# One attention and mixture-of-experts kernel: VectorE's order of gates, value differences and make-ahead work, and the place of the last key and value loads

## The chip, the core and the metric

The kernel runs on one core of a Trainium2 chip. The metric is the device time of one execution in microseconds; the median of several runs is compared. Five engines work side by side, each in the order in which its instructions were issued: TensorE (PE: matrix products, with PEld for its weight loads), VectorE (DVE), ScalarE (ACT), GpSimd (POOL) and SyncE (SP, here only the issuer of most DMAs). They wait for each other by semaphores.

## The reference

Two sequences of 2048 tokens with 512 features are normalised. One branch is causal attention over them, the other a mixture of 8 experts of which each token uses 2. The output joins both:

```
xn = layernorm(x)
q, k, v = split(layernorm(xn)*gamma + beta) @ qkv          # 512 each
s  = softmax(causal(q @ k.T / sqrt(512))) @ v @ o_proj + xn
g  = silu(sum over the 2 best experts e of  gate_e * (silu(xn @ w1_e.T + b1_e) @ w2_e.T + b2_e))
out = x + s * g
```

## The kernel before

**Stages.** All products are float32. The first stage (about 0 to 300 us) normalises, folds the weights into `wqk` and `wvo`, and writes keys `kt_d`, queries `qt_d` and values `v_d` to memory. The second (about 300 to 632 us) sorts tokens by expert, runs the experts and writes their outputs to `y_d`. The third (632 us to the end) is the attention and the final joining; the change lies there.

**The attention loop.** The main loop at the end of the kernel runs over steps `s`. There are NT = 32 tiles of 128 queries; `seq` orders them (sequence 0 from the last tile to the first, then sequence 1 in a mixed order that ends with its longest tiles). Keys and values stand in blocks of 512; `b` counts them, 0 to 3 for sequence 0 and 4 to 7 (`K` to `K + 3`) for sequence 1. Step s does, in the order in which the instructions are issued:

- scores of tile s on PE, one bank of PSUM for each block of keys (`chunk_scores`, L836). After each block DVE takes its maximum (L842), and then one of the previous tile's `join_p` copies (L924);
- `end_scores` makes the negative maximum `nm` of the tile (L854), `exponentials` has ACT exponentiate (L908), POOL split the result into 16-bit halves `pu` (L912) and SP turn them by DMA (`puT`, L917). The joins of the next step put the halves together to `pT`;
- `fetch_parts` issues loads on SP's queue, at most four a step: `parts_b` lists them by their step, keys (`fetch_k`), values (`fetch_v`) and queries (`fetch_q`), each key or value block in four parts of 256 KB;
- `gate(k)` (L1094, L1095): four DVE operations that weigh the experts' rows for two tiles, and a Silu on ACT (L1099). The rows come by POOL's `gather_y` (L1083);
- the product of probabilities and values, two steps behind the scores.

At the head of later steps `attended` scales a product (ACT L1104, DVE L1107) and `emit` multiplies with the gate and adds x on POOL (L1115, L1116). For the last two tiles (`AHEAD`), `make_ahead` (L1127 to L1129) prepares factors on DVE, and `emit_ahead` uses them.

**Two ways to multiply by the values.** Pairs of tiles not in `FAST` use `values(s)` (L942): products on PE alone. The pairs in `FAST` (pairs 0 to 3 and 13 to 15) use a scheme of the Strassen-Winograd kind with seven products for two tiles. It needs differences of the values, `combine_v` (L967: t1 to t4 for each block), and sums of the probabilities, `combine_p` (L986: s1, s3, s2, s4). `values_first` makes p12 and o1, `values_next` makes p57, both in the even step; `values_end`, in the odd step, makes p64 and p03. Between these products DVE adds parts (`add`, L1011). All of p12, p57, p64 and p03 are banks of one pool with three buffers (`ps_b`). In the odd step:

```
chain(p64[:, LO], s2, vt(s, 1))
add(u2, p64[:, LO], p1)        # DVE, reads the left half of p64
...
chain(p64[:, HI], a22, vt(s, 3), stop=False)
```

So PE's last chain in a pair writes the half of a bank whose other half the first `add` reads.

**Order.** The order is written by hand: the program is issued inside a manual schedule, and what is issued first on an engine runs first on it. In step 2, `combine_p` makes the value differences of all four blocks of sequence 0, each kind right after the sum with its number. Those of sequence 1 come in steps 20, 22, 26 and 29 (`combine`). The gate of pair k comes in step k + 3 (28: step 30; 30: step 31).

Of the kernel before, what the change touches and what calls it, by code (L numbers as in the profile page):

```python
# [26 lines left out]
def gated_attention_moe(  # L27
# [31 lines left out]
    NT = B * S // P  # L59
# [818 lines left out]
    for i in range(NS):  # L878
        experts_step(i)
        if i >= 8 and i % 2 == 0 and early:  # L880
            f, b, c = early.pop(0)
# [73 lines left out]
    def combine_v(b, parts=(1, 2, 3, 4)):  # L955

        n = 1 if b % NBB == NBB - 1 else 2
        v = avs[b].rearrange("p (i h) d -> p i h d", h=2)[:, :n]
        if 1 in parts:
            avts[b] = cp.tile(  # L960
                [P, n, 4, D // 2], F32, name=f"vT_{b}", tag=f"vT{n}", bufs=(1 if n == 1 else NBB - 1)
            )
        t1, t2, t3, t4 = (avts[b][:, :, i, :] for i in range(4))
        b11, b12, b21, b22 = (v[:, :, h, c] for h in range(2) for c in (LO, HI))
        for i, dst, x1, x2 in (1, t1, b12, b11), (2, t2, b22, t1), (3, t3, b22, b12), (4, t4, b21, t2):
            if i in parts:
                nc.vector.tensor_tensor(dst, x1, x2, ALU.subtract)  # L967

    def combine_p(s, blocks=()):


        m = min(place_keys(s), place_keys(s + 1)) // 2
        assert m < 2 * NBB
        a1, a2 = (
            turned[s + i][:, : 2 * m * P].rearrange("p (k h q) -> p k h q", h=2, q=P)
            for i in range(2)
        )
        a11, a12, a21, a22 = a1[:, :, 0], a1[:, :, 1], a2[:, :, 0], a2[:, :, 1]
        s1, s2, s4 = (
            cp.tile([P, 2 * NBB - 1, P], F32, name=f"s{i}_{s}", tag=f"s{i}")[:, :m] for i in (1, 2, 4)  # L980
        )
        for i, dst, x1, x2, op_ in (
            (1, s1, a21, a22, ALU.add), (3, a21, a11, a21, ALU.subtract),
            (2, s2, s1, a11, ALU.subtract), (4, s4, a12, s2, ALU.subtract),
        ):
            nc.vector.tensor_tensor(dst, x1, x2, op_)  # L986
            for b in blocks:
                combine_v(b, (i,))
        combos[s] = m, a11, a12, a22, s1, s2, a21, s4

    def chain(dst, a, v, stop=True):
# [36 lines left out]
    def values_next(s):  # L1028
        _, _, _, _, s1, _, s3, _ = combos[s]
        p57 = bank(s, "p57")  # L1030
        chain(p57[:, LO], s1, vt(s, 0))
        chain(p57[:, HI], s3, vt(s, 2))
        seven[s] += (p57,)
# [45 lines left out]
    def gather_y(s):  # L1079
        n = seq[s]  # L1080
        for k in range(2):
            y = op.tile([P, D], F32, name=f"yg{k}_{s}", tag=f"yg{k}")
            nc.gpsimd.indirect_dma_start(  # L1083
                out=y, out_offset=None, in_=y_d,
                in_offset=bass.IndirectOffsetOnAxis(ap=posi[k][:, n : n + 1], axis=0),
            )
            rows[s, k] = y

    def gate(s):

        g = op.tile([P, 2, D], F32, name=f"g_{s}", tag="g", bufs=2)
        for i in range(2):
            w = [share[k][:, 0, seq[s + i] : seq[s + i] + 1] for k in range(2)]
            nc.vector.tensor_scalar(g[:, i, :], rows.pop((s + i, 0)), w[0], None, ALU.mult)  # L1094
            nc.vector.scalar_tensor_tensor(  # L1095
                g[:, i, :], rows.pop((s + i, 1)), w[1], g[:, i, :], ALU.mult, ALU.add
            )
            gates[s + i].append(g[:, i, :])
        nc.scalar.activation(g, g, AF.Silu)  # L1099
# [23 lines left out]
    def make_ahead(s):  # L1123
        xt, g = gates[s]
        n = seq[s]
        w = op.tile([P, D], F32, name=f"w_{s}", tag="w", bufs=1)
        nc.vector.tensor_scalar(w, g, xscale[:, n : n + 1], 1.0, ALU.mult, ALU.add)  # L1127
        nc.vector.tensor_tensor(xt, xt, w, ALU.mult)
        nc.vector.scalar_tensor_tensor(  # L1129
            xt, g, xshift[:, n : n + 1], xt, ALU.mult, ALU.add  # L1130
        )

    def emit_ahead(s, o, cols):
# [9 lines left out]
    K = NBB  # L1143
    parts_b = [(0, fetch_v, 0), (0, fetch_v, 1), (1, fetch_v, 2), (1, fetch_v, 3),
               (4, fetch_k, K + 2), (6, fetch_v, K + 2), (8, fetch_k, K + 1), (10, fetch_v, K + 1),
               (12, fetch_k, K), (14, fetch_v, K), (16, fetch_k, K + 3), (18, fetch_v, K + 3)]
    parts_b = [(s, f, b, c) for s, f, b in parts_b for c in range(ND)]
    parts_b += [(2 * n - 2 * NQ + 2, fetch_q, n, c) for n in range(NQ, NT // 2) for c in range(2)]
    parts_b.sort(key=lambda part: part[0])
# [9 lines left out]
    for s in range(NT + OUT + 2):  # L1159
        fast = s // 2 - 1 in FAST  # L1160
        if s < NT and s:
            begin_scores(s)
        if s == 1:
            fetch_parts(s, 2 * ND)
        for k in range(NT):
            if k not in AHEAD:
                wait = 4 - k % 2 if k // 2 in FAST else 3
                if s == k + wait:
                    attended(k)
                if s == k + wait + 1:  # L1170
                    emit(k)
        for k in range(NT):
            if s == (NT - 1 if k in AHEAD else k + 2 - k % 2 if k // 2 in FAST else k + 1):
                fetch_inputs(k)
        joins = []
        if 0 <= s - 1 < NT - 1:
            joins = [(join_p, s - 1, j) for j in range(len(widths[s - 1]))]
        if s < NT:
            for j in range(len(widths[s])):
                if s:  # L1180
                    chunk_scores(s, j)
                if joins:
                    f, *args = joins.pop(0)
                    f(*args)
        for f, *args in joins:
            f(*args)
        if s < NT and s:
            end_scores(s)
        if fast and s % 2 == 0 and s < NT:
            combine_p(s - 2, range(NBB) if s == 2 else ())  # L1190
        if 0 <= s - 1 < NT:
            divisor(s - 1)
        if s < NT:
            exponentials(s)
            fetch_parts(s, 4 if s else 2 * ND)
            if s in combine:
                combine_v(combine[s])

        for k in range(0, NT, 2):
            if s == (k + 1 if k in AHEAD else k + 2 if k + 2 in AHEAD else k + 3):  # L1200
                gate(k)
        for k in range(0, NT, 2):
            if s == (k if k in AHEAD else k + 1):
                gather_y(k)
                gather_y(k + 1)
        if s == NT - 1:
            for k in AHEAD:
                make_ahead(k)
        if fast and s % 2 == 0:
            values_first(s - 2)  # L1210

            if s != NT - 2:
                values_next(s - 2)
        elif fast and s == NT - 1:
            values_next(s - 3)
            values_end(
                s - 3,
                [lambda j=j: join_p(s, j) for j in range(len(widths[s]))] + [lambda: combine_p(s - 1)],
            )
        elif fast:  # L1220
            values_end(s - 3)
        elif 0 <= s - 2 < NT:
            values(s - 2)
    att.close()


# [42 lines left out]
```

## Time and profile before

| what | value |
|---|---|
| median of 3 runs | 1093.47 us (1091.65 to 1094.91) |
| the profiled execution's own time | 1094.23 us |
| its span, first to last instruction | 1092.5 us |
| granted clock of TensorE | 0.998 of full speed |
| PE busy | 1068.2 us, 98% |
| DVE busy | 556.1 us, 51% |
| POOL busy | 401.8 us, 37% |
| ACT busy | 328.9 us, 30% |
| DMA | 210.08 MB, 192 GB/s in the mean |

Times in the profile are counted from the span's start. A row of a timeline gives start, length, engine, line, operation, the tile written and read, the count of merged instructions and, in square brackets, how long the engine stood idle before it and what it waited for. In the list of waits a row gives the waiting engine and line, what it waited for, the microseconds in total, how often, and the longest. A float32 product appears as two matmul instructions.

### The profile page before, as it was taken

How to read it: one execution, taken by the hardware profiler on the slowest of the kernel's cores; microseconds unless marked ns; L12 is line 12 of the kernel's file. 1: busy time of each engine (PE TensorE's matmuls, PEld its weight loads, DVE VectorE, ACT ScalarE, POOL GpSimd, SP SyncE). 2: the span in 40 equal slices, each digit the busy share in tenths (PEclk: the TensorE clock that was granted, in tenths of full speed). 3: DMA queues.
4: the chain of work that ended last, by engine and by line, in shares of the span. 5: the costliest groups of instructions: out<-in, count | busy, mean ns of one | idle time of the engine just before them, and what ended most of it. 6: DMA issues, size and time to landing. Idle time of an engine off the chain costs nothing.

```text
span 1092.5 us, 11592 instructions
## 1 busy us (share of the span) xinstructions
PE 1068.2 (98%) x3326; PEld 575.9 (53%) x3326; DVE 556.1 (51%) x1102; ACT 328.9 (30%) x689; POOL 401.8 (37%) x443
## 2 busy tenths in 40 slices
PE   8999999999999999999999999999999999999998
PEld 3444444444555555555545446676654444546567
DVE  4634441686333333333345338555565558675675
ACT  3232423211333232323256231221233333432230
POOL 2411120002433333333331023353557577673342
PEclk9999999999999999999999999999999999999999
DMA  8989879935999999999985175455668796663451
GB/s 298 250 248 285 253 229 333 307 108 139 183 255 224 228 226 226 236 223 232 207 187 148 34 226 143 90 123 150 156 185 211 221 240 194 177 164 89 98 127 38
DMA packets 306509, 210.08 MB, mean 192 GB/s; under 512 B 238088, under 2 KB 250888, under 8 KB 305424
## 3 DMA queue, kind: packets, MB, share of 16 engines
q1 hardware_dynamic: 284368, 146.91, 54.5%
q0 software_dynamic: 10560, 35.17, 12.7%
q10 hardware_dynamic: 11520, 27.27, 6.7%
q8 instruction: 28, 0.46, 0.2%
q14 instruction: 33, 0.27, 0.1%
HBM read 92.89 MB, written 60.03 MB: 140 GB/s over the span
## 4 chain that ended last, share of the span: by engine, by line
PE 80%; issue 6%; DVE 5%; POOL 5%; ACT 2%; DMA 2%; ACTq 0%; POOLq 0%; DVEq 0%
PE ps L836 15%; PE py L791 15%; PE ph L752 15%; PE pj L324 10%; PE pj L329 9%; PE p L994 8%; PE pw L200 3%; PE po L942 3%; POOL yg L1083 2%; POOL o L1115 1%; DMA puT<-pu 1%; PE p L942 1%; DVE g L1094 1%; POOL o L1116 1%; PE pg L290 1%
## 5 line engine op out<-in xcount | busy, mean ns | idle before, releaser
L836 PE MATMUL ps<-k,q 128*128 128x512 f32 (+3 forms) x640 | 239.1, 529 | 0.0
L791 PE MATMUL py<-w,ht 128*128 (+3 forms) x408 | 187.0, 594 | 0.0
L836 PEld LDWEIGHTS ps<-k,q 128*128 128x128 f32 x640 | 117.9, 190 | 121.8 <-issue 111.7
L752 PE MATMUL ph<-w,xT 128*128 (+1 forms) x544 | 173.1, 460 | 0.7 <-POOL keep L874 0.7
L912 POOL COPY pu<-pr 128x1024 uint16<-128x1024 uint16 (+3 forms) x80 | 89.3, 1142 | 198.5 <-ACT pr L908 177.6
L777 ACT ACTIVATE ht<-ht,b1sel 128x128 f32<-128x128 f32 (+3 forms) x237 | 73.1, 375 | 230.6 <-DVE ht L771 230.6
L752 PEld LDWEIGHTS ph<-w,xT 128*128 128x128 f32 (+1 forms) x544 | 97.5, 181 | 73.0 <-issue 33.1
L799 DVE COPY y<-py 128x512 f32<-128x512 f32 x68 | 46.9, 690 | 173.7 <-PE py L791 173.7
L762 POOL COPY hu<-h 128x704 uint16<-128x704 uint16 x68 | 52.5, 772 | 206.7 <-ACT h L760 153.4
L324 PE MATMUL pj<-kT,wqk 128*128 128x512 f32 x256 | 113.2, 595 | 0.0
L791 PEld LDWEIGHTS py<-w,ht 128*128 128x128 f32 (+3 forms) x408 | 73.6, 182 | 75.1 <-issue 38.3
L329 PE MATMUL pj<-wvo,kT 128*128 128x512 f32 x256 | 113.0, 595 | 0.0
L638 POOL DMA_INDIRECT xs<-zu_d,toki x68 | 69.4, 1020 | 69.3 <-DVE toki L538 57.9
L908 ACT ACTIVATE pr<-ps,nm 128x512 f32<-128x512 f32 (+3 forms) x80 | 49.0, 620 | 151.4 <-DVE ri L1067 137.9
L842 DVE TENSOR_REDUCE mx<-ps 128x1 f32<-128x512 f32 (+3 forms) x80 | 48.7, 609 | 78.6 <-PE ps L836 77.4
L942 PE MATMUL po<-v,pT 128*128 128x512 f32 x182 | 83.1, 604 | 5.0 <-DVE ri L1067 2.8
L334 ACT COPY j<-pj 128x512 f32<-128x512 f32 x64 | 37.3, 583 | 141.6 <-PE pj L324 66.7
L324 PEld LDWEIGHTS pj<-kT,wqk 128*128 128x128 f32 x256 | 47.7, 190 | 59.1 <-issue 54.9
L247 POOL COPY zu<-z 128x1024 uint16<-128x1024 uint16 x32 | 36.1, 1129 | 115.4 <-DVE z L232 115.4
L329 PEld LDWEIGHTS pj<-wvo,kT 128*128 128x128 f32 x256 | 47.8, 190 | 57.9 <-issue 55.4
L1083 POOL DMA_INDIRECT yg<-y_d,posi x64 | 66.3, 1035 | 18.4 <-issue 13.3
L924 DVE COPY pT<-puT 128x1024 uint16<-128x1024 uint16 (+3 forms) x80 | 58.3, 736 | 28.1 <-DMA puT<-pu 27.9
(183 smaller groups left out, 1190.8 us busy)
## 6 DMA issues: line engine op xcount, KB each, us to landing
y_d<-y SPq DMA_DIRECT2D x68, 256.0 KB, 3.7
zu_d<-zu SPq DMA_DIRECT2D x32, 264.0 KB, 3.8
x<-in_x_dram SPq DMA_DIRECT2D x32, 256.0 KB, 4.8
kt_d<-kT ACTq DMA_DIRECT2D x8, 1024.0 KB, 4.4
qt_d<-j ACTq DMA_DIRECT2D x32, 256.0 KB, 3.2
v_d<-j ACTq DMA_DIRECT2D x32, 256.0 KB, 3.4
k<-kt_d SPq DMA_DIRECT2D x32, 256.0 KB, 4.3
q<-qt_d SPq DMA_DIRECT2D x32, 256.0 KB, 4.6
```

Of the source, the lines that this page charges most:

```text
L324: nc.tensor.matmul(po, lhsT=wqk[:, c, ts(r, P)], rhs=kT[:, c, :], start=(c == 0), stop=(c == ND - 1),)
L329: nc.tensor.matmul(po, lhsT=kT[:, c, ts(r, P)], rhs=wvo[:, c, :], start=(c == 0), stop=(c == ND - 1),)
L638: nc.gpsimd.indirect_dma_start(out=xs, out_offset=None, in_=zu_d, in_offset=bass.IndirectOffsetOnAxis(ap=toki[:, i : i + 1], axis=0),)
L752: nc.tensor.matmul(ph[at, :], lhsT=xT[:, c, at], rhs=rhs[k], start=(c == 0), stop=(c == ND - 1),)
L777: nc.scalar.activation(ht[:hn, c, at], ht[:hn, c, at], AF.Silu, bias=b1sel[:hn, c, j : j + 1])
L791: nc.tensor.matmul(py[at, :], lhsT=ht[:k, c, at], rhs=rhs[n], start=(c == 0), stop=(c == NH - 1),)
L836: nc.tensor.matmul(ps[:, :w], lhsT=aqs[seq[s] // 2][:, c, ts(t % 2, P)], rhs=aks[first + j][:, c, :w], start=(c == 0), stop=(c == ND - 1),)
L912: nc.gpsimd.tensor_copy(pu[:, : 2 * w].rearrange("p (h d) -> p h d", h=2), pr[:, :w].bitcast(U16).rearrange("p (d h) -> p h d", h=2),)
L924: nc.vector.tensor_copy(turned[s][:, j * TB : j * TB + w].bitcast(U16).rearrange("p (i t h) -> p i t h", t=P, h=2), halves[s][j][:, : 2 * ...
L942: nc.tensor.matmul(dst, lhsT=turned[s][:, ts(k, P)], rhs=avs[first + k // BT][:, k % BT, cols], start=(start and k == k0), stop=(k == k1 - 1),
L994: nc.tensor.matmul(dst, lhsT=a[:, k], rhs=v(k), start=(k == 0), stop=(stop and k == n - 1))
L1083: nc.gpsimd.indirect_dma_start(out=y, out_offset=None, in_=y_d, in_offset=bass.IndirectOffsetOnAxis(ap=posi[k][:, n : n + 1], axis=0),)
```

## The change

It moves four things and adds or removes no instruction of the computation:

- the first differences t1 of the values of sequence 0 leave `combine_p` and are made in step 2 between the maxima: blocks 0 and 1 after the second block's maximum and join, 2 and 3 after the third's and fourth's;
- in steps with a pair of `FAST`, the gate is issued behind the value products and their adds instead of ahead of them; in the last score step (31) it stays ahead of `values_end`, but behind `values_next`, and `make_ahead` goes behind `values_end`;
- `gather_y`, which follows the gate, stays behind it;
- the loads of the last block of keys move from step 16 to step 20, those of the last block of values from step 18 to step 22. The query loads queued behind them come a step earlier.

```diff
@@ combine_p
             nc.vector.tensor_tensor(dst, x1, x2, op_)
             for b in blocks:
-                combine_v(b, (i,))
+                if i > 1:
+                    combine_v(b, (i,))
@@ parts_b
-               (12, fetch_k, K), (14, fetch_v, K), (16, fetch_k, K + 3), (18, fetch_v, K + 3)]
+               (12, fetch_k, K), (14, fetch_v, K), (20, fetch_k, K + 3), (22, fetch_v, K + 3)]
@@ main loop, after each chunk_scores and its join
+                if s == 2 and j:
+                    for b in (0, 1) if j == 1 else (j,):
+                        combine_v(b, (1,))
@@ main loop, after exponentials and fetch_parts
-        for k in range(0, NT, 2):
-            if s == (k + 1 if k in AHEAD else k + 2 if k + 2 in AHEAD else k + 3):
-                gate(k)
-        for k in range(0, NT, 2):
-            if s == (k if k in AHEAD else k + 1):
-                gather_y(k)
-                gather_y(k + 1)
-        if s == NT - 1:
-            for k in AHEAD:
-                make_ahead(k)
         if fast and s % 2 == 0:
             values_first(s - 2)
 
             if s != NT - 2:
                 values_next(s - 2)
         elif fast and s == NT - 1:
             values_next(s - 3)
+            gate(s - 1)
             values_end(
                 s - 3,
                 [lambda j=j: join_p(s, j) for j in range(len(widths[s]))] + [lambda: combine_p(s - 1)],
             )
+            for k in AHEAD:
+                make_ahead(k)
         elif fast:
             values_end(s - 3)
         elif 0 <= s - 2 < NT:
             values(s - 2)
+
+        for k in range(0, NT - 2, 2):
+            if s == (k + 2 if k + 2 in AHEAD else k + 3):
+                gate(k)
+        for k in range(0, NT, 2):
+            if s == (k if k in AHEAD else k + 1):
+                gather_y(k)
+                gather_y(k + 1)
```

## The prediction

> **What bounds the kernel now.** First the page's first two parts: TensorE (PE) is busy over 98% of the span and its clock is granted in full, so time can only come out of PE's gaps. The list of what PE waited for names them:
>
> ```profile
> PE 1068.2 (98%) x3326; PEld 575.9 (53%) x3326; DVE 556.1 (51%) x1102; ACT 328.9 (30%) x689; POOL 401.8 (37%) x443
> PE p L994 <- DVE u L1011: 5.6, 4, 2.6
> PE po L942 <- DVE ri L1067: 2.8, 1, 2.8
> PE p L994 <- DVE vT L967: 2.3, 4, 0.9
> PE po L942 <- DVE pT L924: 2.2, 3, 1.0
> ```
>
> Two of these waits, for u and for vT, are on the very instructions that the change moves others away from. PE's timeline places them (steps s are recognised by the widths of their scores):
>
> ```profile
> 663.90 1.03 PE L942 MATMUL p<-v,pT 128*128 128x256 f32 x4
> 665.86 1.10 PE L994 MATMUL p<-vT,s 128*128 128x256 f32 x4 [0.93 <-DVE vT L967]
> 671.00 3.29 PE L994 MATMUL p<-vT,pT 128*128 128x256 f32 x14 [0.79 <-DVE vT L967]
> ...
> 1008.48 0.60 PE L942 MATMUL p<-v,pT 128*128 128x256 f32 x2
> 1011.71 2.43 PE L994 MATMUL p<-vT,pT 128*128 128x256 f32 x10 [2.64 <-DVE u L1011]
> ...
> 1058.29 0.59 PE L942 MATMUL p<-v,pT 128*128 128x256 f32 x2
> 1060.59 2.86 PE L994 MATMUL p<-vT,pT 128*128 128x256 f32 x12 [1.71 <-DVE u L1011]
> ```
>
> [...] in a run without gaps the next row starts 0.216 us per 256-wide matmul later (10 in 2.16 us). By that pitch a gap is up to 0.2 us more than its bracket says. VectorE's (DVE's) timeline shows what stands ahead of the two late instructions:
>
> ```profile
> 1009.83 0.48 DVE L1094 TENSOR_SCALAR g<-yg,share 128x512 f32<-128x512 f32 x1
> 1010.35 0.98 DVE L1095 SCALAR_TENSOR_TENSOR g<-yg,share,g 128x512 f32<-128x512 f32 x1
> 1011.25 0.41 DVE L1011 TENSOR_TENSOR u<-p,p 128x256 f32<-128x256 f32 x1
> ...
> 660.67 0.69 DVE L924 COPY pT<-puT 128x1024 uint16<-128x1024 uint16 x1 [1.37 <-DMA puT<-pu]
> 664.17 4.75 DVE L967 TENSOR_TENSOR vT<-v 128x512 f32<-128x512 f32 x4
> ...
> 900.27 0.43 DVE L924 COPY pT<-puT 128x512 uint16<-128x512 uint16 x1 [3.53 <-DMA puT<-pu]
> 908.69 1.02 DVE L924 COPY pT<-puT 128x1024 uint16<-128x1024 uint16 x1 [2.18 <-DMA puT<-pu]
> ```
>
> The first u add reads a product that PE finished at about 1005.5, but it starts at 1011.25, after the gate; PE's next chain starts at its end. In step 2 DVE idles 1.37 us at 660.67, then spends 4.75 us on the first value differences while PE waits.
>
> [...] the last chain (right half of p64) waits for the u add (left half): the trace agrees, 1011.66 against 1011.71. [...] the same gate operation takes 0.49 us or 1.26 us, the latter beside POOL's pu copies. [...] Here a transpose issued at 891.84, behind the last values, reached DVE at 900.27; the median is 3.3 us.
>
> **The change, part by part.** No instruction is added or removed; all is order.
>
> 1. *First differences of the values (step 2).* Four subtractions leave combine_p. They go between maxima: DVE is at the second join by 658.6, with 1.37 + 0.54 us idle before the later joins. Free of POOL's copies (which start at 664.1) they cost 3 x 0.67 + 0.41 = 2.4 us, not 4.75. The value loads end issuing at 650.76 and land in 5.6 us, by 657, so no new wait. Maxima, nm and exponentials of step 2 come about 0.6 us later, in front of transposes whose copies have 10 us in hand. Then s1 ends near 664.8, s3 near 666.5, and the third differences run 666.5 to 670.1, still beside POOL's copies. PE's first chain goes at 664.93 without a gap; the second, from 667.95, may wait 0.2 us inside. Before it started at 671.00. Worth 3.05 at most (671.00 - 667.95); I take **2.85**, bounds 1.5 and 3.05.
>
> 2. *Gates behind the adds in steps 3, 5, 7, 9, 29.* A gate is four DVE operations, 2.5 us alone, 3.9 us beside POOL. Without them in front, u is read as soon as its product is there. By the pitch PE loses 0, 0, 0.38 (768.04 to 768.42), 1.25 (796.51 to 797.76) and 2.80 (1008.91 to 1011.71). In step 29 the four differences of the last block stay in front and end at 1007.95; u then ends at 1008.4, 0.5 us ahead of need. All goes: **4.43**, bounds 3 and 4.43.
>    What is late instead: the gate, then its Silu on ScalarE (1.06; its table load of 1.28 doesn't wait and is hidden), then two attended activations in ACT's order (0.81 each), then DVE's last multiply-add (0.75): 6 to 7.3 us in front of the next step's first maximum. The cover is that step's scores: 10.3 us in step 4, 8.6 in step 6, 6.9 in step 8, 5.2 in step 10, 12.9 in step 30. Step 8: nm comes 0.7 to 2 us later, s1 with it at 781.5 to 782.9, and PE wants it at 782.3: cost 0 to 0.6. Step 10: nm 2.5 to 4 us later, but its values are multiplied at 825.8 and its copies were made at 816.3: 8 us to spare. POOL's gathers wait for the gates' reads and end some 4 us later; POOL next works 12 us after their old end in step 3 (698.5 to 710.7) and 6.7 us after it in step 9. I take **0**, bound 2.5.
>
> 3. *Last steps.* In step 31 the gate stays ahead of the adds, but six make_ahead operations (1055.57 to 1060.20), which waited 4.11 us for the Silu, go behind. PE's last chain starts at 1058.72 instead of 1060.59: **1.87**. Next in line: four joins and four combinations, ready for the product at 1068.6 with 5 us to spare; make_ahead then ends near 1071.2 and the add that frees the bank of p12 near 1074.4, PE wants that bank at 1077.7. Step 30's gate goes behind one add; nothing waits there. Bounds 0.5 and 1.87.
>
> 4. *Last keys and values, steps 16 and 18 to 20 and 22.* Four 256 KB loads each, 1.95 us of SyncE's (SP's) queue each; two query loads each move a step earlier. SP had time (last transpose of step 19 issued as its copy ended), [...] the 8.4 us transpose behind the values holds DVE at 900.27, hence the maxima, exponentials and transposes of step 20, and the join at 908.69 for which PE loses 1.14 (908.71 to 909.85). Without it that join comes near 905. At the new places the loads follow the transposes of their step and precede those of steps 21 and 23, whose joins have 4 and 5 us to spare once the lateness is gone; the data is needed only at step 28. **1.14**, bounds -1.5 and 2.
>
> 5. *Steps 10 to 27 otherwise.* values() is PE alone, so swapping it with the gate changes no engine's order: **0**. The 2.81 us wait at 846.87 (a transpose behind another key load) and two of 0.5 to 0.7 us stay: this stretch follows PE step by step, so earlier gains shift it whole.
>
> Sum 2.85 + 4.43 + 1.87 + 1.14 = 10.3 us. The profiled execution took 1094.23 (span 1092.5), 0.76 above the median of the runs, so 1083.9 for it and **1083.2** against 1093.47. A measurement here can tell about 0.3%, 3.3 us, from no change.
>
> **Rivals.**
> - *Part of it comes back.* The gate's chain is not fully covered in steps 8 and 10 (0.6 + 2.5), the value differences win half (1.5) and the loads nothing: about 10.3 - 3.1 - 1.35 - 1.14 = 4.7 gained, 1088.8. For it: contended gates of 3.9 us, the margin of s1 under 1 us. Against: the exponentials' long way to the product.
> - *Absorbed.* Steps 10 to 22 hang on POOL and the DMA engines (the chain of waits runs through POOL from 800 to 900); if they can't start earlier, what steps 2 to 9 win (4.5) is lost, and a load that still collides takes 1.14 and more: gain near 3, 1090.5, no change. Against: POOL idles 2 to 7 us before most copies.
> - *Slower.* The gate's late chain decides: gates, Silu, attended, maxima, with POOL's gathers behind. It costs a step what its cover lacks. Were it uncovered in steps 6, 8 and 10, 3 x 6.9 = 20.7 against 10.3, 1103.9. It decides once more than 13.6 us are uncovered in all, 4.5 us for each of the three; the covers of 5 to 9 us speak against.
> - *It doesn't do what it says*: in 9 of the 16 pairs the gate's move changes no order, as said.
>
> **How the numbers follow.** My forecast (gain 8 to 11.5) 0.64; part comes back (4 to 8) 0.22; absorbed or about none 0.07; slower 0.07. Part comes back and the forecast are both faster by over 0.3%, most of the former's range with them, hence 0.87, 0.06 and 0.07. The range reaches from 1080.5 (all upper bounds, and 1.5 us of spread between runs) to 1088.5, where most of the second case is in.
>
> **What would show it.** Right: no wait of PE for vT at step 2 and none for u; value differences of 0.67 us between maxima; the join of step 20 some 3 us earlier and no wait in front of the product of 14; gates right after the last add of steps 3 to 9. Wrong: new waits of PE for s or pT in steps 8 to 12, DVE standing on v in step 2, or transposes of steps 21 and 23 that land late. The prediction fails if PE's gaps merely move to other lines.

## The result and the profile after

The changed kernel takes **1084.89 us** (median of 4 runs, 1083.99 to 1087.13), the kernel before 1094.19 us in the same series (4 runs, 1091.65 to 1097.05). The ratio is **0.9917**, 95% interval 0.9888 to 0.9947: some 9.1 us faster, between 5.8 and 12.3. The profiled execution took 1085.04 us with a span of 1083.3 us, against 1094.23 and 1092.5.

From here on, lines of the changed kernel behind L986 have numbers higher by one: L994 is L995, L1011 is L1012, the gates are L1095 and L1096, `attended` is L1108. First the page's busy times, after the change:

```profile
PE 1065.3 (98%) x3326; PEld 575.9 (53%) x3326; DVE 548.6 (51%) x1102; ACT 327.9 (30%) x689; POOL 399.0 (37%) x443
```

The same counts of instructions as before: only the order differs. DVE is 7.5 us less busy, 7.0 of it in the two lines of the gate, which no longer runs beside POOL's copies so often (means of 663 and 857 ns, 800 and 939 before). Then the list of PE's waits in the changed kernel (total, how often, longest), the rows for the attention:

```profile
PE po L942 <- DVE ri L1068: 3.3, 1, 3.3
PE po L942 <- DVE pT L924: 2.3, 2, 2.1
PE p L995 <- DVE s L986: 0.6, 1, 0.6
PE p L995 <- DVE vT L967: 0.3, 1, 0.3
```

The wait for u (5.6 us before) is gone; of the 2.3 us for vT 0.3 is left; a new one for s, 0.6, has appeared. PE's timeline of the changed kernel in the steps 2, 29 and 31:

```profile
662.52 1.03 PE L942 MATMUL p<-v,pT 128*128 128x256 f32 x4
664.15 3.26 PE L995 MATMUL p<-vT,s 128*128 128x256 f32 x14 [0.60 <-DVE s L986]
667.41 1.13 PE L995 MATMUL p<-vT,pT 128*128 128x256 f32 x4
668.86 2.58 PE L995 MATMUL p<-vT,pT 128*128 128x256 f32 x10 [0.31 <-DVE vT L967]
...
1004.17 0.60 PE L942 MATMUL p<-v,pT 128*128 128x256 f32 x2
1004.60 2.32 PE L995 MATMUL p<-vT,pT 128*128 128x256 f32 x10
...
1051.08 0.59 PE L942 MATMUL p<-v,pT 128*128 128x256 f32 x2
1051.51 2.75 PE L995 MATMUL p<-vT,pT 128*128 128x256 f32 x12
```

In the last two pairs the chain that stood behind a wait of 2.64 and 1.71 us now starts 0.43 us after the start of the row ahead of it (two matmuls): no gap. In step 2 the first chain still waits 0.60 us, and not for vT but for s1. VectorE's timeline of the changed kernel shows why, and where the gates and the joins now stand:

```profile
655.60 0.69 DVE L924 COPY pT<-puT 128x1024 uint16<-128x1024 uint16 x1 [6.82 <-DMA puT<-pu]
...
657.45 1.28 DVE L967 TENSOR_TENSOR vT<-v 128x512 f32<-128x512 f32 x2
...
662.02 0.59 DVE L924 COPY pT<-puT 128x768 uint16<-128x768 uint16 x1 [0.61 <-DMA puT<-pu]
...
665.84 4.31 DVE L967 TENSOR_TENSOR vT<-v 128x512 f32<-128x512 f32 x4
...
693.46 0.42 DVE L1012 TENSOR_TENSOR o<-p,u 128x256 f32<-128x256 f32 x1 [2.70 <-PE p L942]
693.80 0.48 DVE L1095 TENSOR_SCALAR g<-yg,share 128x512 f32<-128x512 f32 x1
694.31 0.75 DVE L1096 SCALAR_TENSOR_TENSOR g<-yg,share,g 128x512 f32<-128x512 f32 x1
...
892.22 1.92 DVE L924 COPY pT<-puT 128x512 uint16<-128x512 uint16 x1
902.14 1.01 DVE L924 COPY pT<-puT 128x1024 uint16<-128x1024 uint16 x1 [2.20 <-DMA puT<-pu]
...
932.01 1.86 DVE L924 COPY pT<-puT 128x1024 uint16<-128x1024 uint16 x1 [1.59 <-DMA puT<-pu]
```

The first differences take 0.64 us each between the maxima, as intended. The first join of step 2 stands 6.82 us for a transpose, as it did before (6.62), and the fourth, behind the differences, still stands 0.61. The gate of step 3 follows the last add. The last join of step 19 (892.22; the joins from here on are named by the step whose scores they carry, and stand in the step after it) no longer waits for its transpose (3.53 us before); in exchange the join of step 23 (932.01) does.

**Where the time came from.** Laying the two traces side by side by the starts of PE's rows gives the gain as it grows:

| up to | before | after | gain so far | by this part |
|---|---|---|---|---|
| second half of p12, step 2 | 657.86 | 656.48 | 1.38 | (earlier stages, not the change) |
| scores of step 3 | 674.13 | 671.27 | 2.86 | 1.48: differences of step 2 |
| scores of step 10 | 800.03 | 795.33 | 4.70 | 1.84: gates of steps 7 and 9 |
| scores of step 28 | 971.02 | 966.71 | 4.31 | -0.39: steps 10 to 27, loads |
| scores of step 30 | 1014.84 | 1007.63 | 7.21 | 2.90: gate of step 29 |
| p12 of step 30's pair, step 31 | 1064.15 | 1054.96 | 9.19 | 1.98: make_ahead |

So 7.8 us of this pair of spans are the change's. The 1.38 us ahead of step 2's products are not: over the 14 traces of this document that row starts between 656.01 and 658.07.

### The profile page after: what moved, and what is told of

Its sections match the earlier page's. It is cut to its first block, busy times and chain, and to the rows that moved or that the text cites. A ratio compares the mean times of both kernels' runs of the same rounds, so it can differ in the third digit from the quotient of the medians.

```text
span 1083.3 us, 11581 instructions
## 1 busy us (share of the span) xinstructions
PE 1065.3 (98%) x3326; PEld 575.9 (53%) x3326; DVE 548.6 (51%) x1102; ACT 327.9 (30%) x689; POOL 399.0 (37%) x443
## 4 chain that ended last, share of the span: by engine, by line
PE 79%; POOL 6%; issue 6%; DMA 3%; DVE 2%; ACT 2%; SPq 1%; ACTq 0%; POOLq 0%; DVEq 0%
PE ph L752 15%; PE py L791 15%; PE ps L836 13%; PE p L995 10%; PE pj L324 10%; PE pj L329 9%; PE pw L200 3%; DMA puT<-pu 2%; PE p L942 2%; POOL yg L1084 2%; POOL pu L912 1%; POOL o L1117 1%; POOL o L1116 1%; PE po L942 1%; PE pg L290 1%
## 5 line engine op out<-in xcount | busy, mean ns | idle before, releaser
L912 POOL COPY pu<-pr 128x1024 uint16<-128x1024 uint16 (+3 forms) x80 | 85.3, 1094 | 175.5 <-ACT pr L908 148.9
L924 DVE COPY pT<-puT 128x1024 uint16<-128x1024 uint16 (+3 forms) x80 | 60.7, 766 | 24.3 <-DMA puT<-pu 24.3
```

The lines of the kernel that those rows point to most:

```text
L912: nc.gpsimd.tensor_copy(pu[:, : 2 * w].rearrange("p (h d) -> p h d", h=2), pr[:, :w].bitcast(U16).rearrange("p (d h) -> p h d", h=2),)
L924: nc.vector.tensor_copy(turned[s][:, j * TB : j * TB + w].bitcast(U16).rearrange("p (i t h) -> p i t h", t=P, h=2), halves[s][j][:, : 2 * ...
```

## Experiments

Each kernel was run in 5 rounds beside the kernel before, and its ratio is to that one; a difference in us is the ratio's distance from 1 times 1094.3. The diffs are cut to what matters.

**The four parts, each alone on the kernel before.**

Part 1 alone:

```diff
@@ combine_p
-                combine_v(b, (i,))
+                if i > 1:
+                    combine_v(b, (i,))
@@ main loop
+                if s == 2 and j:
+                    for b in (0, 1) if j == 1 else (j,):
+                        combine_v(b, (1,))
```

> The kernel before, with only the first value differences moved between the maxima of step 2. Theory (each wait of PE is worth its own time): PE keeps a wait of about 0.8 us for s1 and 0.6 to 0.9 us for the third differences, as in the changed kernel, so the gain is about 1.5 us of the 3.05 that PE lost there, and 0.1% of the time. Rival (the differences hide whole, and the 1.5 us seen was the accident of one execution): 2.85 us. Rival (absorbed by the stretch from step 10 to 22): PE reaches step 3 earlier, and the span ends as before. The other waits of PE (5.6 us for u in total) stay in all cases.

Measured: 1092.74 us, ratio 0.9988 (0.9975 to 1.0), a gain of 1.3 us with 0 to 2.7 in its interval. The trace of this run shows the wait for vT down to 0.3 us. The size fits the 1.48 us of the table, half of the 2.85 predicted. But in this run's own trace PE's first chain had no gap at all:

```profile
662.88 1.03 PE L942 MATMUL p<-v,pT 128*128 128x256 f32 x4
663.74 3.19 PE L995 MATMUL p<-vT,s 128*128 128x256 f32 x14
```

So one pair of traces is not enough here. From the second half of p12 to the scores of step 3, the five traces in which step 2 has the old order took 16.27 us (before), 17.20, 17.11, 17.32 and 17.54 (gates, make_ahead, loads, gate behind the first add); the five in which it has that of the changed kernel took 14.79 (the changed kernel), 13.79 (part 1), 14.25, 15.26 and 15.63 (old loads, gates twice, spread loads). The means are 17.1 and 14.7: 2.3 us, within the interval of this run. The trace of the kernel before happens to be the shortest of its order.

Parts 2 and 3 alone. In the first, gates and gathers of steps 3, 5, 7, 9 and 29 are issued behind `values_end`; in the second, `make_ahead` alone goes behind it:

```diff
@@ e2: main loop
+        late = fast and s % 2 and s < NT - 1
+        if not late:
+            gates_now()          # gate(k), gather_y(k), gather_y(k + 1) as before
...
         elif fast:
             values_end(s - 3)
+            if late:
+                gates_now()
@@ e3: main loop, step NT - 1
-            for k in AHEAD:
-                make_ahead(k)
...
             values_end(
...
             )
+            for k in AHEAD:
+                make_ahead(k)
```

> The kernel before, with only the gates (and the gathers behind them) of steps 3, 5, 7, 9 and 29 moved behind the adds. Theory: 1.7 us by step 10 and 2.8 to 2.9 in step 29, about 4.5 us in all; of PE's waits for u only that of step 31 (1.7 us) is left. Rival (the gate's chain of Silu, attended work and maxima comes late in steps 8 and 10): a new wait of PE for s or pT there, and 1.5 to 3 us less gained. Rival (absorbed): 1.7 us of it lost between steps 10 and 22, gain 2.8.

> The kernel before, with only make_ahead moved behind values_end in step 31. Theory: PE's last chain of that pair starts 1.9 us earlier, nothing later waits, gain 1.9 us, the whole of it at the end of the span where nothing can absorb it. Rival (make_ahead is late for the bank of p12 or for the last outputs): a wait of PE in step 33 or a longer tail, gain under 0.5 us.

Measured: the gates 1088.87 us, ratio 0.995 (0.9936 to 0.9964), 5.5 us; make_ahead 1092.6 us, ratio 0.9982 (0.9971 to 0.9993), 2.0 us. The waits of PE for u in the gates' run and in make_ahead's run:

```profile
PE p L994 <- DVE u L1011: 1.7, 1, 1.7
```

```profile
PE p L994 <- DVE u L1011: 3.9, 3, 2.6
```

The first keeps only step 31's wait, the second all but that one: each edit takes away exactly the waits that it was meant for.

Part 4 alone:

```diff
-               (12, fetch_k, K), (14, fetch_v, K), (16, fetch_k, K + 3), (18, fetch_v, K + 3)]
+               (12, fetch_k, K), (14, fetch_v, K), (20, fetch_k, K + 3), (22, fetch_v, K + 3)]
```

> The kernel before, with only the last key and value loads moved to steps 20 and 22. Theory: the join of step 19 no longer waits 3.5 us, the join of step 20 comes some 3 us earlier, PE's wait of 1.0 us before the product of 14 goes, and one of 0.25 us in front of the product of step 23 appears: gain 0.9 us. Rival (the collision only moves): the wait comes back whole at step 21 or 23, gain 0. The waits for vT (2.3) and u (5.6) stay.

Measured: 1095.24 us, ratio 1.0008 (0.9999 to 1.0017). The loads win nothing, and may cost up to 1.9 us. The opposite edit, on the changed kernel:

```diff
-               (12, fetch_k, K), (14, fetch_v, K), (20, fetch_k, K + 3), (22, fetch_v, K + 3)]
+               (12, fetch_k, K), (14, fetch_v, K), (16, fetch_k, K + 3), (18, fetch_v, K + 3)]
```

> The changed kernel, with the last key and value loads back in steps 16 and 18. Theory (from the run of the loads alone: their move wins 0.6 to 1.2 us at step 20 and loses as much at step 23 and before): the same time as the changed kernel within 1 us, PE's wait of 1 us before the product of 14 in step 22 back. Rival (the move is worth its 1.1 us once the earlier waits are gone): 1.1 us slower than the changed kernel, 8 us faster than before. Rival (the move costs, as the loads alone suggest): 1 us faster than the changed kernel.

Measured: 1085.3 us, ratio 0.9923 (0.9907 to 0.9939), the same as the changed kernel within the intervals. PE's timeline of this run, in front of the product for which 1.14 us were lost before:

```profile
903.27 6.25 PE L942 MATMUL po<-v,pT 128*128 128x512 f32 x14 [0.32 <-DVE pT L924]
```

With the other parts in place, that wait is 0.32 us even with the loads where they were: its size changes from trace to trace. All traces together show what the move does. In the six with the old places PE waits 0 to 2.26 us (1.1 in the mean) in front of the product of 14, in step 22, and not at all in front of that of 8, in step 25. In the eight with the new places it waits 0.25 to 2.01 us (1.2 in the mean) in front of the product of 8, and 0.29 or nothing in front of that of 14. The run with early differences, below, is one of the eight:

```profile
934.08 3.67 PE L942 MATMUL po<-v,pT 128*128 128x512 f32 x8 [1.64 <-DVE pT L924]
```

The wait moves, and keeps its size.

**Does PE wait for all adds, or only for the one that frees its bank?** On the kernel before, the gate goes behind the first add alone, with the other adds still behind it:

```diff
@@ values_end
         add(u2, p64[:, LO], p1)
+        if after_first:
+            after_first()        # the gate and its gathers
         add(u3, p57[:, HI], u2)
```

> The kernel before, with the gates (and gathers) of steps 3, 5, 7, 9 and 29 put behind the first add alone: u2 goes ahead of the gate, the other adds of the pair stay behind it. Theory (PE waits only for the read that frees the bank of p64): the whole gain of the gates behind all adds, 4.5 to 5.5 us, and one wait for u left (step 31, 1.7 us). Rival (the adds as a whole are late for PE, through the banks of p57 and p03 too): the wait moves to the first product of the next step and the gain is under 2 us.

Measured: 1088.58 us, ratio 0.9953 (0.9936 to 0.997), 5.1 us, the same as all adds ahead of the gate (5.5). VectorE's timeline of this run in step 9, and PE's (in this kernel the gate's lines are L1096 and L1097):

```profile
793.38 0.42 DVE L1011 TENSOR_TENSOR u<-p,p 128x256 f32<-128x256 f32 x1
793.71 0.48 DVE L1096 TENSOR_SCALAR g<-yg,share 128x512 f32<-128x512 f32 x1
...
797.39 0.42 DVE L1011 TENSOR_TENSOR u<-p,u 128x256 f32<-128x256 f32 x1
```

```profile
795.33 1.03 PE L942 MATMUL p<-v,pT 128*128 128x256 f32 x4
796.19 1.89 PE L994 MATMUL p<-vT,pT 128*128 128x256 f32 x8
```

PE's last chain starts at 796.19, while DVE is still in the gate; the second add comes at 797.39. Of the adds, only the read of the bank that the chain writes held PE here.

**How much room has the late gate?** The changed kernel with the gates of pairs 0, 2, 4, 6 and 26 computed twice, 2.5 us more on DVE behind the adds of steps 3, 5, 7, 9 and 29:

```diff
@@ gate
             gates[s + i].append(g[:, i, :])
+            if s in (0, 2, 4, 6, 26):
+                nc.vector.tensor_scalar(g[:, i, :], ys[0], w[0], None, ALU.mult)
+                nc.vector.scalar_tensor_tensor(
+                    g[:, i, :], ys[1], w[1], g[:, i, :], ALU.mult, ALU.add
+                )
```

> The changed kernel, with the four VectorE operations of the gate done twice in steps 3, 5, 7, 9 and 29 (same result): 2.5 us more of VectorE work behind the adds at each place. Theory (covered by the next step's scores until PE needs its first sum): steps 4, 6, 10 and 30 pay nothing; in step 8 the first sum, 1.3 us ahead of need now, comes 1.2 us late: 1 to 1.5 us slower than the changed kernel, so still 7 to 8 us faster than before. Rival (the chain behind the gate is already at its limit): 2.5 us at each of steps 6, 8 and 10, so only 1 to 2 us faster than before.

Measured: 1088.74 us, ratio 0.9947 (0.9928 to 0.9966): some 3.3 us slower than the changed kernel by the ratios, more than expected. PE's timeline of this run, in steps 2, 8 and 25:

```profile
665.46 3.26 PE L995 MATMUL p<-vT,s 128*128 128x256 f32 x14 [1.06 <-DVE s L986]
...
781.63 1.99 PE L995 MATMUL p<-vT,s 128*128 128x256 f32 x8 [1.20 <-DVE s L986]
...
938.48 5.37 PE L942 MATMUL po<-v,pT 128*128 128x512 f32 x8 [2.01 <-DVE pT L924]
```

Step 8 waits 1.20 us for s1. In the changed kernel s1 stood ready 1.3 us ahead of need there (its end at 777.65, PE's chain at 778.96), so 2.5 us more give 1.2: the chain through gate, Silu and `attended` is real, and its room in the narrowest step is 1.3 us. The other two waits are not where gates were added: step 2 comes ahead of all of them, and the wait in step 25 is the one that every trace with the moved loads has. That one has a second cost here (8 matmuls in 5.37 us instead of 3.67), a half clock as in the last experiment. Such stretches account for most of the rest: the three runs with the mean granted clock of the changed kernel's four runs (0.998) took 1086.7 us in the mean against 1085.2, 1.4 us more and near the 1.2 of step 8; the other three, with 0.995 to 0.997, took 1089.9 to 1091.3.

**What limits step 2?** The changed kernel, with t1 and t3 of the first two blocks made right behind step 2's first maximum, in the time in which DVE stands for the first transpose:

```diff
@@ combine_p
-                if i > 1:
+                if i in (2, 4) or i == 3 and b > 1:
                     combine_v(b, (i,))
@@ main loop, behind chunk_scores, ahead of the join
+                if s == 2 and j == 0:
+                    for b in range(2):
+                        combine_v(b, (1, 3))
...
-                if s == 2 and j:
-                    for b in (0, 1) if j == 1 else (j,):
-                        combine_v(b, (1,))
+                if s == 2 and j > 1:
+                    combine_v(j, (1,))
```

> The changed kernel, with the first and third value differences of blocks 0 and 1 made in step 2 right after the first maximum, where VectorE stands idle for 6.8 us waiting for the turned probabilities; those of block 2 and 3 stay (first kind between maxima, third kind behind its sum). Theory (in step 2 PE loses 1.6 us to VectorE's own work): 0.8 us of wait for s1 and the wait for vT go, 1.3 to 1.6 us faster than the changed kernel, no wait of PE for s or vT in step 2. Rival (the values have not landed yet): VectorE stands on v, the maxima come later, 0 or slower. Rival (absorbed by steps 10 to 22): the waits go and the time stays.

Measured: 1083.95 us, ratio 0.9904 (0.9887 to 0.992): ahead of the changed kernel by 1.4 us in the ratio and 0.9 in the median, with intervals that overlap. VectorE's and PE's timelines of this run:

```profile
649.71 3.73 DVE L967 TENSOR_TENSOR vT<-v 128x512 f32<-128x512 f32 x4
656.90 0.69 DVE L924 COPY pT<-puT 128x1024 uint16<-128x1024 uint16 x1 [3.46 <-DMA puT<-pu]
```

```profile
665.39 3.26 PE L995 MATMUL p<-vT,s 128*128 128x256 f32 x14 [0.83 <-DVE s L986]
668.49 3.19 PE L995 MATMUL p<-vT,pT 128*128 128x256 f32 x14
```

Four differences fit in front of the first join and PE's second chain runs without a gap. The wait for s1 stays, 0.83 us: it hangs less on the differences than on the joins. Two things could hold those: the transposes, queued behind 4 MB of value loads on SP, or POOL's fourth copy, which stands for a free `pu` buffer. A fourth buffer tells them apart:

```diff
-            pu = php.tile([P, 2 * TB], U16, name=f"pu_{s}_{j}", tag="pu")
+            pu = php.tile([P, 2 * TB], U16, name=f"pu_{s}_{j}", tag="pu", bufs=4)
```

> The changed kernel, with four instead of three buffers for POOL's halves pu. Theory (in step 2 VectorE hangs on the fourth join, and that on POOL's fourth copy, which waits 5.5 us for a pu buffer until the first transpose has landed behind the 4 MB of values): the wait of POOL goes, the fourth join of step 2 comes about 1 us earlier, PE's wait of 0.6 us for s1 goes: 0.6 to 1 us faster than the changed kernel, step 2 losing under 1 us instead of 1.6. Rival (the fourth join hangs on the transposes' own rate behind the values, not on the buffer): the join stays at 5.5 us after the start of the first product of step 2, and the time is the same.

Measured: 1086.45 us (1083.35 to 1090.63), ratio 0.9934 (0.9911 to 0.9958), no gain. The timelines of POOL, VectorE and PE in this run:

```profile
648.25 3.78 POOL L912 COPY pu<-pr 128x1024 uint16<-128x1024 uint16 x4 [11.12 <-ACT pr L908]
652.18 0.99 POOL L1084 DMA_INDIRECT yg<-y_d,posi  x1
```

```profile
663.90 0.69 DVE L924 COPY pT<-puT 128x1024 uint16<-128x1024 uint16 x1 [2.34 <-DMA puT<-pu]
```

```profile
667.87 4.95 PE L995 MATMUL p<-vT,s 128*128 128x256 f32 x14 [3.29 <-DVE s L986]
```

POOL's four copies run in one row, where the version with early differences has the fourth at 657.00; but the third join now waits, 2.34 us, and PE with it, 3.29. So the buffer was not what kept PE waiting; in this run the joins stand for transposes that land late. POOL, free earlier, issues its gathers at 652.18 and not at 658.43, beside these transposes; that they are what makes the transposes later was not tried.

**The wait of step 15.** It is the longest that is left. The changed kernel with the load of keys K spread over steps 12 and 13 and that of values K moved from step 14 to 15:

```diff
-               (12, fetch_k, K), (14, fetch_v, K), (20, fetch_k, K + 3), (22, fetch_v, K + 3)]
-    parts_b = [(s, f, b, c) for s, f, b in parts_b for c in range(ND)]
+               (12, fetch_k, K), (15, fetch_v, K), (20, fetch_k, K + 3), (22, fetch_v, K + 3)]
+    parts_b = [(s + (f is fetch_k and b == K and c > 1), f, b, c) for s, f, b in parts_b for c in range(ND)]
```

> The changed kernel, with the key loads of block K split, two parts in step 12 and two in step 13, and its value loads moved from step 14 to 15. Theory (the transpose of step 13 lands 7 us after its issue because 1 MB of keys is ahead of it, and PE waits 3.3 us for it in step 15): the wait of PE for ri in step 15 falls to 1.5 us or less, 1 to 2 us faster than the changed kernel. Rival (the DMA engines are full from 835 to 845 anyway: gathers, queries and outputs): the wait stays within 0.5 us, or comes back in step 16 as a wait for keys, and the time is the same.

Measured: 1086.56 us, ratio 0.993 (0.9911 to 0.9948). No gain, as the rival had it (in the changed kernel the DMA share is 1.07 from 835 to 845); PE's timeline of this run still has the wait in step 15:

```profile
843.99 4.15 PE L942 MATMUL po<-v,pT 128*128 128x512 f32 x6 [3.29 <-DVE ri L1068]
```

All three diffs together, early differences, four buffers and spread loads:

> The changed kernel, with the differences of blocks 0 and 1 in the idle time of step 2, four pu buffers, and the key and value loads of block K spread over steps 12, 13 and 15. Theory: the gains of the three add, 0.9 (measured for the first) and about 0.6 and 1.5: 2.5 to 3.5 us faster than the changed kernel, and 1.1% faster than before. Rival (clock and DMA accidents of one execution decide differences of this size): within 1 us of the run with the differences alone.

Measured: 1085.12 us (1082.84 to 1092.73), ratio 0.9919 (0.9899 to 0.994), with a wait of 4.45 us for s1 in step 2, long as with the four buffers alone. The early differences alone have the lower median, 1083.95 us, though the intervals overlap; nothing is gained by adding the other two.

**Half a clock after a long wait.** The product of step 18 in the changed kernel took 9.69 us for 18 matmuls; at the pitch of other rows it takes 7.99. PE's timeline of the changed kernel, and then stretches of 2 us (length; busy time of PE, PEld, DVE, ACT and POOL; granted clock; DMA share; GB/s):

```profile
867.36 9.69 PE L942 MATMUL po<-v,pT 128*128 128x512 f32 x18 [2.08 <-DVE pT L924]
```

```profile
866.00:868.00 2.00, 0.64 (x2) 0.41 (x3) 2.00 (x3) 0.00 (x0) 0.75 (x1) 1.00 0.46 86
868.00:870.00 2.00, 2.00 (x5) 0.73 (x4) 1.93 (x8) 0.47 (x1) 0.00 (x0) 0.60 0.96 297
870.00:872.00 2.00, 2.00 (x4) 0.90 (x3) 1.97 (x3) 1.98 (x7) 1.63 (x2) 0.54 0.56 202
```

Behind the wait of 2.08 us the granted clock is a half for 3.413 us, from 868.41 to 871.82, and the row loses 1.7 us. The trace of each of the first 13 kernels, before and after among them, has one to three such stretches ahead of PE's last product. Where a trace has two, their starts lie whole multiples of 3.413 us apart: in the run with four buffers 177.49 us, 52.0 times; and in the kernel before and the changed one, where another begins behind the last product, 245.76 and 215.04 us, 72.0 and 63.0 times. So time is cut here into windows of 3.413 us from the start of a stretch at half clock, a grid for counting, and PE's idle time summed in each of them, over the windows that the 13 traces show at full clock, from 0.8 us of idle time up (two stretches went on for a second window, 6.83 us):

| PE idle in one window of 3.413 us | windows | followed by a half clock |
|---|---|---|
| 0.8 to 1.69 us | 41 | 0 |
| 1.70 to 1.74 us | 7 | 1 |
| 1.85 to 3.41 us | 20 | 20 |

In these traces it was not the length of a wait that counted but what of it fell into one window: the wait of 3.28 us in step 15 of the changed kernel is cut into 1.74 and 1.54 us and has no half clock behind it, that of 2.08 us lies in one window and has. To test this, two products were put into the two longest waits of the version with early differences:

```diff
@@ values
         po = ps_b.tile([P, D], F32, name=f"po_{s}", tag="b")
+        if s in (13, 16):        # the steps 15 and 18
+            t, first = seq[s + 2], place(s + 2)[2]
+            for c in range(2):
+                nc.tensor.matmul(
+                    po, lhsT=aqs[t // 2][:, c, ts(t % 2, P)], rhs=aks[first][:, c, :],
+                    start=True, stop=True,
+                )
         product(po, s, 0, place_keys(s), slice(0, D))
```

> The version with the early differences, plus two extra products (4 matmuls of 128x512, about 1.73 us) in front of `values` in steps 15 and 18; they use keys and queries already there, write the bank that `values` then starts anew, and change no result. Theory: TensorE's half-clock stretch of 3.41 us (one to two before the last product in each of the 13 traces so far) [...] in the 13 traces every window with 1.85 us of waiting or more was followed by one and none with less than 1.7. The two long waits, 2 to 3.3 us in step 15 and 1 to 2.7 us in step 18, then shrink to at most 1.6 us, and no half-clock stretch is left before the last product; PE's own work loses nothing, since the extra products lie in waits. The time is 1082.0 to 1083.8 us against a before of 1094.4 (ratio 0.9887 to 0.9903), and the runs lie closer together than those of the changed kernel (3.1 us from lowest to highest). Rival, that the half clock comes by chance or from long full load: at least one stretch is there again, anywhere, and the time is 1084 to 1087 us, the extra products being paid wherever a wait is shorter than they are.

Measured: **1083.6 us** (1083.32 to 1084.69), ratio 0.9901 (0.9885 to 0.9916). PE's timeline of this run:

```profile
839.16 1.88 PE L934 MATMUL po<-k,q 128*128 128x512 f32 x4
841.42 2.84 PE L949 MATMUL po<-v,pT 128*128 128x512 f32 x6 [0.38 <-DVE nm L854]
...
864.38 1.88 PE L934 MATMUL po<-k,q 128*128 128x512 f32 x4
866.82 7.99 PE L949 MATMUL po<-v,pT 128*128 128x512 f32 x18 [0.55 <-DVE pT L924]
```

The extra products lie in the waits, 0.38 and 0.55 us of which are left; the longest gap of the attention stage is 1.37 us; the product of step 18 takes 7.99 us; and no half clock is left ahead of the last product, for the first time in 14 traces (the mean granted clock is 1.000). The other four runs of this version have mean clocks of 0.999 to 1.000, the four of the changed kernel 0.998. The runs lie within 1.4 us, those of the changed kernel within 3.1 and those with early differences alone within 2.5. The median gained little over early differences alone (1083.95), because there the half clock of step 15 had been made up by a shorter wait in step 18: its product starts at 866.97 in one and 866.82 in the other. This version is 1.0% faster than the kernel before; its median is 1.3 us below that of the changed kernel, with intervals that overlap, and it is not told apart in time from the early differences alone.

## Why the prediction was right

The forecast was 1083.2 us with a range of 1080.5 to 1088.5; measured were 1084.89. Against the kernel before in the same series the gain is 9.1 us, against a sum of 10.3. By its steps:

1. **First differences: mechanism right, size too large.** 2.85 taken, bounds 1.5 and 3.05; 1.48 in this pair of traces, 1.3 (0 to 2.7) alone, 2.3 by the means of five traces of each order. The step that failed is that the transposes were taken to land as in the one trace. In the changed kernel's trace s1 ended at 664.0; that trace runs 1.38 us earlier, so 665.4 on the scale of before, 0.6 behind the "s1 ends near 664.8". The differences of three blocks lay in idle time as forecast, for DVE still stood 0.61 us behind them. But the fourth join came at 662.02, 663.4 on the scale of before, 0.8 later than in the kernel before:

```profile
662.57 0.56 DVE L924 COPY pT<-puT 128x768 uint16<-128x768 uint16 x1 [0.54 <-DMA puT<-pu]
```

In the ten traces DVE stands 0 to 1.75 us in front of that join. PE's first chain "goes without a gap" in two of the five with the new order (part 1 alone, old loads) and waits 0.60 to 1.43 us in the other three. A second loss is in all five: PE's second chain waits inside for the third differences, which take 4.31 us beside POOL's copies; the prediction allowed 0.2 us for it. The run with early differences shows idle time that could have been used: ahead of the first join. It and the version with extra products took 14.0 and 13.7 us for the stretch that took 14.7 in the mean.
2. **Gates: right, and perhaps worth more than their waits.** 4.43 taken, 4.74 in the traces (0.49, 1.35 and 2.90), 5.5 alone (3.9 to 7.0). A possible reason for more: before the change, the 2.64 us of step 29 can have a half clock behind them. Two of the four traces with that wait show it whole in one window, as in PE's timeline of the run with the loads alone:

```profile
1012.53 4.11 PE L994 MATMUL p<-vT,pT 128*128 128x256 f32 x10 [2.64 <-DVE u L1011]
```

In the kernel before this row took 2.43; 1.68 us are added. In a third trace (part 1 alone) 2.15 us of the wait lie in one window, with the same result; only in that of before is it cut into 1.44 and 1.20. An estimate from the table above, with the windows lying anywhere: a wait of 2.64 us has no half clock behind it only if the cut leaves less than 1.71 on both sides, 0.78 us of 3.41, 23%. That would be 0.77 x 1.68 = 1.3 us more in the mean, so 4.43 + 1.3 = 5.7 against 5.5 measured. This is not shown: the interval holds 4.43 as well, and the mean clock of the gates' six runs, 0.9973, is no higher than that of the kernel before in 53 runs, 0.9975; the gates' trace has its half clocks in steps 2 and 15. What is shown is that the prediction read "its clock is granted in full" from a mean of 0.998, and so left out a cost that a wait can have behind it.
The late chain through gate, Silu and `attended` cost nothing, as taken; the doubled gates put its room in step 8 at 1.3 us, where the prediction had it between 0.8 and -0.6.
3. **make_ahead: right.** 1.87 taken, 1.98 in the traces, 2.0 alone. Neither the joins nor the bank of p12 became late.
4. **Loads: wrong in effect.** 1.14 taken; alone the edit lost 0.9 us (-0.1 to 1.9), and undoing it in the changed kernel cost 0.4 us by the medians, within the intervals. The first half was right: "that join comes near 905" is 905.6 when the 3.41 us gained by then are added to 902.14, and PE's product of 14 waits no more (909.85 to 905.23 in its start, 1.21 beyond that gain). The step that failed is that the joins of steps 21 and 23 "have 4 and 5 us to spare". The join of step 23 now waits 1.59 us for a transpose issued behind the moved value loads, and PE waits 0.25 us for it in this trace, up to 2.01 in the seven others with these loads and never in the six without: 1.2 us in the mean, against 1.1 in front of the product of 14 before. The wait moved and did not vanish.
5. **Steps 10 to 27:** the net is -0.39 us, loads included. The changed kernel gains 1.1 us in step 15, where the kernel before has a half clock, loses 3.1 in step 18 (2.08 us of waiting with a half clock behind it), gains 0.7 in step 19, whose wait of 0.51 us is gone, and 1.4 around the product of 14, and loses 0.5 in step 25. The long wait of step 15 stayed, as said.

The sum thus fails by 1.1 to 2 in part 4 and by 0.5 to 1.5 in part 1, and parts 2 and 3 give back up to 1.2: that the total came so near is in part luck. Of the rivals, "part of it comes back" was right for the loads (at nothing) and, by the run alone, for the value differences (at half), but not for the gates. "Absorbed" is refuted by the table: of the 4.70 us gained by step 10, 4.31 are there in step 28. The slower one is refuted by the doubled gates: even 2.5 us more in that chain uncovered 1.2 us in one step.

Open: why three of the six runs with doubled gates have more half clocks than the runs of the changed kernel; and what sets the landing of the transposes in step 2 and in step 25, which changes from execution to execution. And whether early differences are faster than the changed kernel (0.9 to 1.4 us) lies within their intervals.

## What to carry to other kernels

PE bounds this kernel and writes a bank that DVE reads; of all adds only the read of that very bank had to come early (with the gate behind it, PE's chain started at 796.19, ahead of the second add at 797.39). So look up which read it is, put it first, and let everything else, a gate or prepared factors, follow. Before work is moved "into idle time", ask what ends that idle time: here the landing of a transpose ended it, at a time that changed by more than a microsecond from execution to execution, so that one pair of traces gave 1.5 us where five gave 2.3. A moved load may carry its wait elsewhere: 1.1 us in front of the product of 14 became 1.2 in front of that of 8. And of TensorE's waits the long ones deserve work first: behind the 2.08 us of step 18 a half clock took another 1.7.

## What the runs showed of the hardware that was not expected

TensorE's granted clock fell to a half for 3.413 us at a time (from 846.67 to 850.08 in the kernel before, from 868.41 to 871.82 in the changed one), in these two traces behind waits of 2.81 and 2.08 us. Counted in windows of 3.413 us, as above, it did so behind 20 of 20 with 1.85 us or more of PE's idle time, none of 41 with less than 1.70, and one of seven between. The price was up to 1.7 us where PE set the pace (9.69 us for the product of step 18 instead of 7.99) and next to nothing where a later wait took it up (early differences: that product at 866.97, against 866.82 with no half clock). Counted from the span's start, the windows begin at another place in each trace (0.16 us beyond whole multiples in the kernel before, 1.42 in the changed one), and the wait of 2.64 us in step 29 had a half clock behind it in three of four traces. That is probably a part of the spread of runs: in the 85 runs of the kernel before that stand beside the experiments, the mean time is 1092.6 us at a mean clock of 1.000 (20 runs), 1093.9 at 0.998 (19), 1095.0 at 0.997 (25) and 1095.6 at 0.995 (21). One stretch takes 0.0016 off the mean clock (half of 3.41 in 1092 us), so by an estimate from these means the runs have none, one, two and three: about 1 us each, of which a part may be the longer waits that bring a stretch on.

A DVE subtraction of two float32 inputs of 128x512 took 0.67 us alone and 1.52 while POOL copied (so the first two of the four in 4.31 us at 665.84). Of the gate's two operations the first took 0.49 us alone and 1.26 beside POOL's copies, the second 0.75 and 1.40.
